# A state-space scan layer: two tiles per scan, decays in SBUF, the carry as a column of the products

## The chip, the cores and the metric

The kernel runs on one core of one Trainium2 chip, as a single launch that computes four image layers one after the other. The metric is the device time of the launch in microseconds (us). A profile of one execution goes with it, taken by the hardware profiler. Its engines are PE (TensorE matrix multiply) with PEld (its weight loads), DVE (VectorE), ACT (ScalarE), POOL (GpSimd) and SP (SyncE, which here only starts DMAs).

## The reference

The input is an image x of 48 channels by 128 x 128 pixels in float32. Each layer normalises x by groups of channels, applies its own operator and adds the result to x: attention over all pixels (layer 0), four directional recurrent sweeps (layer 1), a patchwise convolution through Fourier transforms (layer 2) and a selective scan (layer 3). Only layer 3 matters here:

```python
# tokens: (1, 4096, D) with D = 192: 48 channels x a 2x2 window of pixels
Bm = tokens @ W_B.T + b_B
Cm = tokens @ W_C.T + b_C
dt = jax.nn.softplus(tokens @ W_dt.T + b_dt)
delta = jax.nn.softplus(dt + b_dt)
A = -jnp.exp(A_log)                       # (D, D)

def step(h, inp):                         # over the 4096 tokens
    d_l, u_l, B_l, C_l = inp
    dA = jnp.exp(d_l[:, :, None] * A[None])
    h = dA * h + (d_l * u_l)[:, :, None] * B_l[:, None, :]
    y = jnp.einsum('bdn,bn->bd', h, C_l)
    return (h, y)
```

So there are 192 x 192 independent first-order recurrences over 4096 tokens: h = decay * h + product, where the decay is exp(delta * A) and the product is (delta * u) * B. The state is then contracted with C over n, and a skip term and a constant factor are added.

## The kernel before

Layers 0 to 2 stand first and are not touched. Layer 3 is the function `scan`. The 4096 tokens are cut into four chunks of LC = 1024. The 192 rows d are handled in Q = 96 pairs: two rows d lie on two halves of 64 partitions each, and the 192 states n are three blocks k of 64. A tile is thus 128 partitions by 1024 tokens for one pair and one k. Three pairs (P = 3) make a group of nine tiles, and there are 32 groups (NG) in each chunk: 128 groups and 1152 tiles in all. The buffer `h` holds the nine tiles of a group; the pool `l3_h` has two such buffers.

The loop over groups runs over nine slots, `p, k = divmod(slot, 3)`. This is what it does for a tile:

- At k = 0, SP loads the broadcast rows `dt` (delta) and `du` (delta times u) of the pair from DRAM, and POOL forms the products of all three k with one instruction, `nc.gpsimd.tensor_mul` at line 1497, which writes `h[:, p, ks]` from `du` and `bt` (the B matrix of the chunk). Both inputs and the output lie in SBUF.
- For each slot, ACT computes the decays, `act.activation(dA, dt, AF.Exp, scale=...)`, into `dA`, which lies in PSUM (pool `ps_a`, two buffers).
- DVE runs the recurrence with `nc.vector.tensor_tensor_scan` at line 1504. It reads `dA` from PSUM and the products from `h` in SBUF, and writes the states over the products. Its initial value is the constant 0.0 in the first chunk and the pointer `carry[:, i, k : k + 1]` in the later ones.

A scan therefore waits for its exponential and for the products of its pair. An exponential waits until the scan of two tiles before has read its PSUM buffer. The products of a group wait until the buffer `h` of two groups earlier has been read by everyone.

The contraction with C is hung into the slots of the following group (`contract`, `late`): at slot 1 PE multiplies the finished tiles of `h` with the placed C matrix `cw` into `y` (192 matmuls for each of two parts), at slot 2 ACT copies the last state column of the group to `carry` (`hand_on`), at slots 6 and 7 ACT copies `y` to `ev`, PE picks rows by `sel`, ACT copies them to `ys` at slots 9 and 10, and a DMA stores them to DRAM. `ev` and `ys` come from the pool `l3_e` with two buffers. In the last chunk `finish` adds the results to the image and writes it out. The work that makes the next chunk ready (`prepare`, `part_steps`) is spread over slots 3 and 8; it uses a tile `dd`. `InOrder` (line 48 issues for it) keeps the instructions of ACT and of PE in the order in which the program names them; DVE and POOL have only the waits.

At the start of the layer, `first` prepares chunk 0. It reads the first part of the image from `const["x3"]`, a tile of SBUF that layer 2 fills and that nothing reads afterwards.

Of the kernel before, what the change touches and what calls it, by code (L numbers as in the profile page):

```python
# [19 lines left out]
F32 = mybir.dt.float32  # L20
F16 = mybir.dt.float16
AF = mybir.ActivationFunctionType
ALU = mybir.AluOpType
# [955 lines left out]
def scan(ctx, tc, x3, const, ins, out):  # L979
# [7 lines left out]
    nc = tc.nc  # L987
    act, pe = InOrder(tc, nc.scalar), InOrder(tc, nc.tensor)
    ident = const["ident"]
    so = const["so"]  # L990
    C2 = 2 * C
    D = 4 * C
    L = CH
    NP = 2
    LC = NP * L
# [4 lines left out]
    P = 3  # L1000
    NG = Q // P
    BK = 16
    NB = L // BK // 4

    wp = ctx.enter_context(tc.tile_pool(name="l3_w", bufs=1))
    ap = ctx.enter_context(tc.tile_pool(name="l3_a", bufs=2))
    sp = ctx.enter_context(tc.tile_pool(name="l3_s", bufs=1))
    hp = ctx.enter_context(tc.tile_pool(name="l3_h", bufs=2))
    bp = ctx.enter_context(tc.tile_pool(name="l3_b", bufs=3))
    ep = ctx.enter_context(tc.tile_pool(name="l3_e", bufs=2))  # L1010
    dram = ctx.enter_context(tc.tile_pool(name="l3_y", bufs=1, space=bass.MemoryType.DRAM))
    dram2 = ctx.enter_context(tc.tile_pool(name="l3_dd", bufs=2, space=bass.MemoryType.DRAM))
    ps_a = ctx.enter_context(tc.tile_pool(name="l3_pa", bufs=2, space=PSUM))
# [30 lines left out]
    nc.gpsimd.memset(cw, 0.0)  # L1044

    carry = wp.tile([128, Q, 3], F32, name="carry")
    yd = dram.tile([D, T], F32, name="yd")
    yu = dram.tile([D, T], F32, name="yu")
    yu_by = yu.rearrange("(c a b) l -> a c b l", a=2, b=2)
# [4 lines left out]
    def prepare(ci):  # L1054
# [8 lines left out]

        def first():

            t = hp.tile([128, P, 3, LC], F32, name="h")[0:C2].rearrange("c p k l -> c (p k l)")
            e, w, dd = t[:, 0 : 2 * LC], t[:, 2 * LC : 4 * LC], t[:, 4 * LC : 8 * LC]
            e, w = (v.rearrange("c (b l) -> c b l", b=2) for v in (e, w))
            dd = dd.rearrange("c (b s l) -> c b s l", b=2, s=2)
            ln = ct[0:C2, 0:2, :]  # L1070
            for part in range(NP):
                us.append(ap.tile([C2, 2, L], F32, name="xn"))
            for part, x in enumerate(us):
                xi = rows(const["x3"][:, part, :]).rearrange("c i (j b) -> c i j b", b=2)
                xo = x.rearrange("c b (i j) -> c i j b", j=64)
                act.activation(xo, xi, AF.Identity, bias=so[:, 1:2], scale=so[:, 0:1])

            def both(lhsT, m):
                t = ps_a.tile([128, LC], F32, name="dA")
                for part, x in enumerate(us):  # L1080
                    for b in range(2):
                        pe.matmul(
                            t[0:m, part * L : (part + 1) * L],
                            lhsT=lhsT(b),
                            rhs=x[:, b, :],
                            start=(b == 0),
                            stop=(b == 1),
                        )
                return t[0:m]

            def split(b, z):
                bias = bdt[:, b : b + 1]
                act.activation(e[:, b], z, AF.Abs, bias=bias)
                nc.vector.tensor_scalar(dd[:, b, 1], z, bias, 0.0, ALU.add, ALU.max)

            def take_both(out, t, bias):
                act.activation(out, t, AF.Identity, bias=bias)

            for again in range(2):
                for b in range(2):  # L1100
                    split(b, dd[:, b, 0] if again else both(lambda i: wdt[:, i, b, :], C2))
                for b in range(2):
                    act.activation(e[:, b], e[:, b], AF.Exp, scale=-1.0)
                    nc.vector.tensor_scalar_add(w[:, b], e[:, b], 1.0)
                for b in range(2):
                    act.activation(ln[:, b], w[:, b], AF.Ln)

                    nc.vector.scalar_tensor_tensor(
                        w[:, b], w[:, b], 1.0, e[:, b], ALU.subtract, ALU.subtract
                    )  # L1110
                    nc.vector.tensor_sub(e[:, b], dd[:, b, 1], w[:, b])
                if again == 0:
                    tables()
                    for k in range(2):
                        take_both(bt[:, k], both(lambda i: wb[:, i, k, :], 128), bb[:, k : k + 1])
                for b in range(2):
                    nc.vector.tensor_add(dd[:, b, 0], e[:, b], ln[:, b])
            take_both(bt[:, 2], both(lambda i: wb[:, i, 2, :], 128), bb[:, 2:3])
            for b in range(2):
                for part, x in enumerate(us):  # L1120
                    cols = slice(part * L, (part + 1) * L)
                    nc.vector.tensor_mul(dd[:, b, 1, cols], dd[:, b, 0, cols], x[:, b, :])
                for i in range(2):
                    half = slice(i * C, (i + 1) * C)
                    (act if i else nc.sync).dma_start(rep_by[i][:, b], dd[half, b])
            for k in (2, 0, 1):
                take_both(ct[:, k], both(lambda i: wc[:, i, k, :], 128), bc[:, k : k + 1])
            for part, x in enumerate(us):
                for b in range(2):
                    act.activation(  # L1130
                        w[:, b, part * L : (part + 1) * L], x[:, b], AF.Copy, scale=dp[:, b : b + 1]
                    )
            for i in range(2):
                act.dma_start(yu_by[i][:, :, 0:LC], w[i * C : (i + 1) * C])
# [142 lines left out]
        if ci == 0:  # L1277
            first()
            for f in placing:
                f()  # L1280
            return {"bt": bt, "rep": rep}, [], []
        else:
            dd0 = sp.tile([C2, 2, 2, L], F32, name="dd")
            steps += part_steps(0) + part_steps(1)

        held = {}
# [29 lines left out]
    def contract(h, g, ci):  # L1316
# [8 lines left out]
        def products(part):  # L1325
            def f():
                y[part] = ps_y.tile([128, NB * P * BK], F32, name="y")
                for q in range(NB):
                    for k in range(3):
                        for j in range(4):  # L1330
                            m = (j * NP + part) * NB + q
                            pe.matmul(
                                y[part][
                                    j * 32 : (j + 1) * 32, q * P * BK : (q + 1) * P * BK
                                ].rearrange("m (p t) -> m p t", t=BK),
                                lhsT=cw[:, k, m, :],
                                rhs=h[:, :, k, m * BK : (m + 1) * BK],
                                start=(k == 0),
                                stop=(k == 2),
                            )  # L1340

            return f

        def hand_on():
            act.copy(carry[:, g * P : (g + 1) * P, :].unsqueeze(3), h[:, :, :, LC - 1 : LC])

        def take(part):
            return lambda: act.copy(ev[:, part], y[part])
# [106 lines left out]
        }  # L1455

    ready, steps, place = prepare(0)
    late = {}
    for ci in range(NCK):
        r = ready  # L1460
        if ci:
            steps = []
        for g in range(NG):
            h = hp.tile([128, P, 3, LC], F32, name="h")
            for slot in range(3 * P):
                p, k = divmod(slot, 3)
                i = g * P + p
# [2 lines left out]
                if (g, slot) == (1, 1):  # L1470
                    while place:
                        place.pop(0)()
                    if ci + 1 == NCK:
                        ct = sp.tile([128, 3, LC], F32, name="ct").rearrange("c k l -> c (k l)")
                        dd = sp.tile([C2, 2, 2, L], F32, name="dd").rearrange(
                            "c b s l -> c (b s) l"
                        )
                        for n in range(4):
                            yy = ct[:, n * 2 * D : (n + 1) * 2 * D]
                            ends.append((yy.rearrange("t (s e) -> t s e", e=D), dd[0:C, n]))  # L1480
# [7 lines left out]
                if k == 0:  # L1488
# [6 lines left out]
                            )  # L1495
                    for ks in [slice(0, 3)] if ci or i else [slice(n, n + 1) for n in range(3)]:
                        nc.gpsimd.tensor_mul(  # L1497
                            h[:, p, ks],
                            du.unsqueeze(1).to_broadcast([128, ks.stop - ks.start, LC]),
                            r["bt"][:, ks],  # L1500
                        )
                dA = ps_a.tile([128, LC], F32, name="dA")
                act.activation(dA, dt, AF.Exp, scale=a[:, k, i : i + 1])
                nc.vector.tensor_tensor_scan(  # L1504
                    h[:, p, k, :],
                    dA,
                    h[:, p, k, :],
                    carry[:, i, k : k + 1] if ci else 0.0,
                    ALU.mult,
                    ALU.add,  # L1510
                )
            late = {n - 3 * P: fs for n, fs in late.items()}
            for n, fs in contract(h, g, ci).items():
                late.setdefault(n, []).extend(fs)
# [232 lines left out]
```

## Time and profile before

| | us |
|---|---|
| median of 3 runs | 7599.12 |
| lowest, highest run | 7595.06, 7599.31 |
| profiled execution | 7597.49 |
| its span, first to last instruction | 7595.7 |
| first product of line 1497 starts | 4924.70 |
| first scan of line 1504 starts | 4935.89 |
| last scan of line 1504 starts | 7573.4 |
| PE busy in the whole span | 6125.8 |
| ACT busy in the whole span | 4410.3 |
| DVE busy in the whole span | 3378.7 |
| POOL busy in the whole span | 2792.3 |

The span is what the profile covers; the device time of the same execution is 1.8 us more. The busy times of the whole span mix four layers with different limits, so a change in layer 3 is read from its own stage, which takes the last third, from about 4925 us to the end. In the cost groups each line gives the source line, the engine, the operation, the tiles written and read, the shapes and the count, then the busy time in us and the mean of one in ns, and after the second bar the idle time of the engine just before such instructions, and what ended it. Line 48 is the helper that issues for ACT and PE, so these are told apart by the names of their tiles.

### The profile page before, as it was taken

How to read it: one execution, taken by the hardware profiler on the slowest of the kernel's cores; microseconds unless marked ns; L12 is line 12 of the kernel's file. 1: busy time of each engine (PE TensorE's matmuls, PEld its weight loads, DVE VectorE, ACT ScalarE, POOL GpSimd, SP SyncE). 2: the span in 40 equal slices, each digit the busy share in tenths (PEclk: the TensorE clock that was granted, in tenths of full speed). 3: DMA queues.
4: the chain of work that ended last, by engine and by line, in shares of the span. 5: the costliest groups of instructions: out<-in, count | busy, mean ns of one | idle time of the engine just before them, and what ended most of it. 6: DMA issues, size and time to landing. Idle time of an engine off the chain costs nothing.

```text
span 7595.7 us, 203249 instructions
## 1 busy us (share of the span) xinstructions
PE 6125.8 (81%) x93756; PEld 3162.8 (42%) x93756; DVE 3378.7 (44%) x2497; ACT 4410.3 (58%) x4868; POOL 2792.3 (37%) x574
## 2 busy tenths in 40 slices
PE   7999999999999999999988889755545545554555
PEld 3333333333333333333367755334334343343444
DVE  8300000000000000000022234499999999999998
ACT  2566666666666666666625003366666667666665
POOL 0000000000000000000000022299999999999998
PEclk9999999999999999999999999876767767776666
DMA  3000000000000000000000011166556665656775
GB/s 66 8 4 4 4 3 4 4 4 3 4 4 3 4 4 4 3 4 4 4 1 17 1 33 37 46 160 165 158 158 167 156 160 154 164 159 164 177 181 150
DMA packets 182350, 484.85 MB, mean 64 GB/s; under 512 B 35859, under 2 KB 67778, under 8 KB 179506
## 3 DMA queue, kind: packets, MB, share of 16 engines
q1 hardware_dynamic: 175471, 464.69, 24.0%
q8 instruction: 735, 12.04, 0.7%
q10 hardware_dynamic: 6019, 7.09, 0.4%
q14 instruction: 125, 1.02, 0.0%
HBM read 428.03 MB, written 22.02 MB: 59 GB/s over the span
## 4 chain that ended last, share of the span: by engine, by line
PE 58%; DVE 24%; issue 7%; POOL 4%; ACT 2%; DMA 1%; SPq 0%; DVEq 0%; POOLq 0%; ACTq 0%
PE s L48 23%; PE acc L48 23%; DVE h L1504 20%; PE p L678 6%; POOL h L1497 3%; PE y L48 2%; DVE xb L48 1%; DVE xa L48 1%; DMA du<-rep 1%; PE pp L48 1%; PE pc L48 1%; PE po L48 1%; ACT dA L48 1%; DVE y L48 0%; POOL y L901 0%
## 5 line engine op out<-in xcount | busy, mean ns | idle before, releaser
L48 ACT ACTIVATE e<-s,absT 128x1024 f32<-128x1024 f32 x2048 | 2279.2, 1115 | 1197.5 <-PE s L48 1196.7
L1497 POOL TENSOR_TENSOR h<-du,bt 128x3072 f32<-128x3072 f32 (+1 forms) x386 | 2560.0, 6672 | 83.2 <-DMA du<-rep 62.1
L48 PE MATMUL s<-xa,xb 49*64 49x512 f32 x16384 | 2133.9, 589 | 10.6 <-DVE xb L271 10.6
L48 PE MATMUL acc<-e,xb 64*64 64x512 f32 x16384 | 2131.9, 588 | 0.0
L1504 DVE TENSOR_TENSOR_SCAN h<-dA,carry,h 128x1024 f32<-128x1024 f32 x864 | 1939.8, 2329 | 43.3 <-ACT dA L48 27.2
L48 ACT ACTIVATE dA<-dt,a 128x1024 f32<-128x1024 f32 x1152 | 1287.3, 1118 | 867.5 <-DVE h L1504 856.4
L48 PE MATMUL y<-h,cw 128*32 128x48 f32 x49152 | 886.2, 244 | 933.2 <-issue 499.0
L366 DVE TENSOR_TENSOR both<-o 128x512 f32<-128x512 f32 x32 | 22.2, 693 | 3078.6 <-ACT o L48 3078.6
L614 POOL MEMSET xa<- 48x128 f32 x1 | 0.3, 326 | 3523.5 <-PE acc L48 3523.5
L48 PEld LDWEIGHTS y<-h,cw 128*32 128x32 f32 x49152 | 796.5, 138 | 1057.8 <-issue 653.1
L48 PEld LDWEIGHTS s<-xa,xb 49*64 49x64 f32 x16384 | 643.9, 132 | 1129.9 <-issue 587.3
L48 PEld LDWEIGHTS acc<-e,xb 64*64 64x64 f32 x16384 | 643.1, 132 | 1118.9 <-issue 1096.0
L1504 DVE TENSOR_TENSOR_SCAN h<-dA,h 128x1024 f32<-128x1024 f32 x288 | 633.9, 2270 | 44.8 <-ACT dA L48 36.0
L48 PE MATMUL yz<-ev,sel 128*8 128x48 f32 x4096 | 193.5, 260 | 280.0 <-ACT ev L48 274.3
L48 PEld LDWEIGHTS yz<-ev,sel 128*8 128x8 f32 x4096 | 162.7, 106 | 338.3 <-ACT ev L48 305.9
L678 PE MATMUL p<-xb,l_w 112*112 112x129 f32 x1524 | 233.6, 289 | 42.6 <-DVE xb L48 42.5
L678 PE MATMUL p<-xa,l_w 112*112 112x129 f32 x1524 | 232.2, 288 | 41.9 <-DVE xa L48 41.9
L699 POOL TENSOR_TENSOR xb<-xb,xa 48x2048 f32<-48x2048 f32 (+2 forms) x10 | 44.7, 4465 | 559.0 <-DVE xa L48 559.0
L678 PEld LDWEIGHTS p<-xb,l_w 112*112 112x112 f32 x1524 | 181.9, 177 | 94.1 <-DVE xb L48 94.1
L661 ACT COPY xa<-xb 48x128 f32<-48x128 f32 x256 | 107.3, 419 | 194.5 <-issue 136.0
L678 PEld LDWEIGHTS p<-xa,l_w 112*112 112x112 f32 x1524 | 180.6, 176 | 93.3 <-DVE xa L48 93.3
L48 PE MATMUL pc<-wt,xa 128*128 128x288 f32 x768 | 198.8, 416 | 7.4 <-DMA xa<-xa 7.4
(186 smaller groups left out, 3349.7 us busy)
## 6 DMA issues: line engine op xcount, KB each, us to landing
du<-rep SPq DMA_DIRECT2D x768, 256.0 KB
dt<-rep SPq DMA_DIRECT2D x768, 256.0 KB
rep<-dd SPq DMA_DIRECT2D x24, 192.0 KB
yd<-ys ACTq DMA_DIRECT2D x256, 12.0 KB
rest<-xa SPq DMA_DIRECT2D x90, 38.0 KB
band<-band SPq DMA_DIRECT2D x8, 414.4 KB
xa<-in_x_dram SPq DMA_DIRECT2D x8, 384.0 KB
rest<-band SPq DMA_DIRECT2D x96, 32.0 KB
```

The lines of the kernel that those rows point to most:

```text
L48: ins = method(*args, **kwargs).ins
L366: nc.vector.tensor_add(self.both, o[:, 0], o[:, 1])
L614: nc.gpsimd.memset(b[64:K, lines, E + W - 1 : E + W], 0.0)
L661: nc.scalar.copy(u[at : at + C, :, y], t[0:C, E + h, E : E + W])
L678: nc.tensor.matmul(p, lhsT=w[0:K, which, i, :], rhs=state[0:K, 2 * i : 2 * i + L], start=False, stop=(i == 2),)
L699: nc.gpsimd.tensor_add(xr, xr, u[0:C, x : x + xr.shape[2], E : E + H].rearrange("c w h -> c h w"),)
L1497: nc.gpsimd.tensor_mul(h[:, p, ks], du.unsqueeze(1).to_broadcast([128, ks.stop - ks.start, LC]), r["bt"][:, ks],)
L1504: nc.vector.tensor_tensor_scan(h[:, p, k, :], dA, h[:, p, k, :], carry[:, i, k : k + 1] if ci else 0.0, ALU.mult, ALU.add,)
```

## The change

Three things are changed in `scan`. One scan instruction now covers two neighbouring tiles of `h`, and a single one is used for the ninth tile of a group and for the first pair of the first chunk. The decays go to two SBUF tiles `dA0` and `dA1` of two times 1 + 1024 columns, used in turn, whose first columns are zero. And each tile of `h` has one more column ahead of its products: ACT copies the carry of the pair there at the start of the group, for all nine tiles in one instruction. At this column the decay is zero, so that the recurrence forgets what came before and takes over the carry, and the scan's initial value is always the constant 0.0. The carry is cleared at the start.

To make room in SBUF, `l3_e` has one buffer instead of two, and `dd` uses the tile `const["x3"]`.

```diff
-    ep = ctx.enter_context(tc.tile_pool(name="l3_e", bufs=2))
+    ep = ctx.enter_context(tc.tile_pool(name="l3_e", bufs=1))
...
     carry = wp.tile([128, Q, 3], F32, name="carry")
+    nc.vector.memset(carry, 0.0)
+    decays = [wp.tile([128, 2, 1 + LC], F32, name=f"dA{i}") for i in range(2)]
+    for t in decays:
+        nc.vector.memset(t[:, :, 0:1], 0.0)
+    dd0 = const["x3"].rearrange("c b (s l) -> c b s l", s=2)
...
-            dd0 = sp.tile([C2, 2, 2, L], F32, name="dd")
...
-                                rhs=h[:, :, k, m * BK : (m + 1) * BK],
+                                rhs=h[:, :, k, 1 + m * BK : 1 + (m + 1) * BK],
...
-            act.copy(carry[:, g * P : (g + 1) * P, :].unsqueeze(3), h[:, :, :, LC - 1 : LC])
+            act.copy(carry[:, g * P : (g + 1) * P, :].unsqueeze(3), h[:, :, :, LC:])
...
-    late = {}
+    late, behind = {}, 0
...
-            h = hp.tile([128, P, 3, LC], F32, name="h")
+            h = hp.tile([128, P, 3, 1 + LC], F32, name="h")
+            act.copy(h[:, :, :, 0:1], carry[:, g * P : (g + 1) * P, :].unsqueeze(3))
...
                         nc.gpsimd.tensor_mul(
-                            h[:, p, ks],
+                            h[:, p, ks, 1:],
                             du.unsqueeze(1).to_broadcast([128, ks.stop - ks.start, LC]),
                             r["bt"][:, ks],
                         )
-                dA = ps_a.tile([128, LC], F32, name="dA")
-                act.activation(dA, dt, AF.Exp, scale=a[:, k, i : i + 1])
-                nc.vector.tensor_tensor_scan(
-                    h[:, p, k, :],
-                    dA,
-                    h[:, p, k, :],
-                    carry[:, i, k : k + 1] if ci else 0.0,
-                    ALU.mult,
-                    ALU.add,
-                )
+                if not behind:
+                    decays.append(decays.pop(0))
+                act.activation(decays[0][:, behind, 1:], dt, AF.Exp, scale=a[:, k, i : i + 1])
+                behind += 1
+
+                if behind == 2 or slot == 3 * P - 1 or not (ci or i):
+                    scanned = h.rearrange("n p k l -> n (p k) l")[:, slot + 1 - behind : slot + 1]
+                    nc.vector.tensor_tensor_scan(
+                        scanned.rearrange("n k l -> n (k l)"),
+                        decays[0][:, 0:behind].rearrange("n k l -> n (k l)"),
+                        scanned.rearrange("n k l -> n (k l)"),
+                        0.0,
+                        ALU.mult,
+                        ALU.add,
+                    )
+                    behind = 0
```

More of the change, by code (lines that the diff above doesn't have):

```diff
@@ L1064, in first @@
         def first():
-            t = hp.tile([128, P, 3, LC], F32, name="h")[0:C2].rearrange("c p k l -> c (p k l)")
+            t = hp.tile([128, P, 3, 1 + LC], F32, name="h")[0:C2].rearrange("c p k l -> c (p k l)")
             e, w, dd = t[:, 0 : 2 * LC], t[:, 2 * LC : 4 * LC], t[:, 4 * LC : 8 * LC]
@@ L1474, in scan @@
                         ct = sp.tile([128, 3, LC], F32, name="ct").rearrange("c k l -> c (k l)")
-                        dd = sp.tile([C2, 2, 2, L], F32, name="dd").rearrange(
-                            "c b s l -> c (b s) l"
-                        )
+                        dd = dd0.rearrange("c b s l -> c (b s) l")
                         for n in range(4):
@@ L1501, in scan @@
                         )
-                dA = ps_a.tile([128, LC], F32, name="dA")
-                act.activation(dA, dt, AF.Exp, scale=a[:, k, i : i + 1])
-                nc.vector.tensor_tensor_scan(
-                    h[:, p, k, :],
-                    dA,
-                    h[:, p, k, :],
-                    carry[:, i, k : k + 1] if ci else 0.0,
-                    ALU.mult,
-                    ALU.add,
-                )
+                if not behind:
[13 more added lines that the diff above has]
+                    behind = 0
             late = {n - 3 * P: fs for n, fs in late.items()}
```

## Prediction

> **What bounds the kernel now.** I read the forty slices first, then the cost groups, then the timeline and the two scan-layer lines by source, and the chain of waits last. The slices give the stage that the change can reach:
>
> ```profile
> PE   7999999999999999999988889755545545554555
> DVE  8300000000000000000022234499999999999998
> ACT  2566666666666666666625003366666667666665
> POOL 0000000000000000000000022299999999999998
> ```
>
> From slice 26 on (26 x 189.9 = 4937 us) it is the scan layer, and it fills both DVE and POOL; ACT is at six tenths and PE at five. The window over this stage says so in numbers (columns: stretch, its length, then busy time and count of PE, PEld, DVE, ACT, POOL):
>
> ```profile
> 4924.70:7569.00 2644.30, 1410.38 (x53780) 1084.58 (x53782) 2566.96 (x1150) 1722.91 (x2048) 2573.93 (x392) 0.69 0.63 164
> 7200.00:7400.00 200.00, 117.05 (x4344) 96.76 (x4338) 200.00 (x90) 125.15 (x150) 197.81 (x31) 0.67 0.70 178
> ```
>
> DVE 2567 and POOL 2574 of 2644 us: two engines side by side, each 97% full. Their instructions:
>
> ```profile
> L1497 POOL TENSOR_TENSOR h<-du,bt 128x3072 f32<-128x3072 f32 (+1 forms) x386 | 2560.0, 6672 | 83.2 <-DMA du<-rep 62.1
> L1504 DVE TENSOR_TENSOR_SCAN h<-dA,carry,h 128x1024 f32<-128x1024 f32 x864 | 1939.8, 2329 | 43.3 <-ACT dA L48 27.2
> L48 ACT ACTIVATE dA<-dt,a 128x1024 f32<-128x1024 f32 x1152 | 1287.3, 1118 | 867.5 <-DVE h L1504 856.4
> L1504 DVE TENSOR_TENSOR_SCAN h<-dA,h 128x1024 f32<-128x1024 f32 x288 | 633.9, 2270 | 44.8 <-ACT dA L48 36.0
> ```
>
> The exponentials wait for the scans (856 us), not the reverse. The timeline from 7197 us (start, duration, instruction, count) gives the spacing, which the means overstate since neighbours overlap:
>
> ```profile
> 7197.42 53.49 POOL L1497 TENSOR_TENSOR h<-du,bt 128x3072 f32<-128x3072 f32 x8
> 7199.07 47.16 DVE L1504 TENSOR_TENSOR_SCAN h<-dA,carry,h 128x1024 f32<-128x1024 f32 x21
> ```
>
> So 53.49/8 = 6.69 us for a product of three tiles, 47.16/21 = 2.246 us for a scan with the carry as a scalar operand. In chunk 0, where the initial value is a constant, the timeline has 18 scans in 39.37 us from 4935.89: 2.187 us. A group of nine tiles is thus 3 x 6.69 = 20.1 us of POOL and 9 x 2.246 = 20.2 us of DVE, in parallel. The last view that matters is how steady a scan is while POOL never rests (minimum/median/maximum in ns):
>
> ```profile
> L1504 DVE TENSOR_TENSOR_SCAN h<-dA,carry,h x864: 2323/2327/2351, 5592.6 to 7573.4; 128x1024 f32<-128x1024 f32 x173
> L1497 POOL TENSOR_TENSOR h<-du,bt x386: 2341/6702/6817, 4924.7 to 7560.1; 128x3072 f32<-128x3072 f32 x191, 128x1024 f32<-128x1024 f32 x2
> ```
>
> The reader is to see that the slowest of 864 scans is 1.2% above the fastest: today the two engines don't touch each other. The chain of waits agrees on what ends last (DVE and POOL each appear as the links):
>
> ```profile
> PE s L48 23%; PE acc L48 23%; DVE h L1504 20%; PE p L678 6%; POOL h L1497 3%; PE y L48 2%; DVE xb L48 1%; DVE xa L48 1%; DMA du<-rep 1%; PE pp L48 1%; PE pc L48 1%; PE po L48 1%; ACT dA L48 1%; DVE y L48 0%; POOL y L901 0%
> ```
>
> [...] in the scan stage every DVE instruction beside a running product is a scan from PSUM. [...] 2187/1024 = 2.14 ns an element, against 1216 ns for a 96x1024 two-input subtraction on DVE.
>
> **The change, part by part.** Profiled execution: 7597.49 us, span 7595.7, so 1.8 us outside it; the median of the runs is 7599.12, 0.02% above, and I predict on the profiled one.
>
> *Scans in pairs.* The built program has 511 scans of 2050 columns and 130 of 1025 in place of 1152 of 1024. [...] Total 511 x 4.325 + 130 x 2.19 = 2210 + 285 = 2495 us, against 2574 busy now. Saved on DVE alone: about 0.7 us a group.
>
> *What POOL makes of it.* The products keep their number, their size and their two inputs; only the output is shifted by one column. By spacing, 383 x 6.68 + 3 x 2.37 = 2565 us, and six products of line 1221, 14 us: 2579 us. Even with DVE free, POOL alone fills the stage. A DVE saving can bring at most the difference of the group times, 20.2 - 20.05, in the 96 groups of chunks 1 to 3: 15 us.
>
> *Decays in SBUF.* This is the term that decides. The scan now reads two SBUF tensors (decays and h), and its partner POOL, which reads du and bt from SBUF, is busy 97% of the time. [...] Then the stage takes the sum and not the maximum: 2579 + 2495 = 5074 us. [...] I take 38 us[...]: 5112 us. POOL starts at 4924.7, so the last scan ends at 10037. The tail after it (7573.4 + 2.33 to 7595.7) stays 20 us: 10057, with 1.8 us outside 10059.
>
> *Edits hidden either way.* The exponentials go to SBUF: 1050 ns for a 96x1024 one there, 1118 ns into PSUM, between -0.07 and +0.1 us each, on an engine with 867 us of idle before them. The 128 copies of the carry column ahead of the products, at 191 ns (as carry<-h), are 24 us of ACT; the copy waits for the matmuls of two groups earlier, long done, and behind it stand exponentials with two pairs of slack. POOL's first product of a group waits, in the built order, for the same matmuls and the same carry<-h copy as now, not for the new copy, so POOL is not tied to ACT. A scan of columns 2 and 3 now waits for the second product of its group; POOL is a product ahead, so nothing. One buffer in place of two for ys and ev: each is free ten slots before its next use. SP's queue is unchanged. Three memsets ahead of line 1094, under 1 us.
>
> **The rivals.**
> *No lock for a scan*[...]. For: the trace can't exclude it. [...] Then POOL is the bound and the gain is the 15 us above, less waits from coarser scans of at most 10: 7585, from 7575 to 7600. This is the side of no slowdown, and it decides if a paired scan lasts 4.4 us beside a running product.
> *The interface is shared access by access.* A group's products read 3 x 3072 x 2 = 18432 values per partition in 20.05 us; if this fills the interface, the scans' 9225 more make 27657 x 20.05 / 18432 = 30.1 us a group, plus 10 us in 128 groups: 1285 us more, 8880. [...]
> *The change does what it says and nothing comes of it* is the first rival's upper half: DVE gets 79 us lighter and POOL, as long as before, sets the end.
>
> **How the numbers follow.** Serialised 0.77, shared 0.09, no lock 0.14. The prediction is the first: 10060 us. Its own range is 9950 to 10260. Leaving out only the no-lock case and the ends, the range runs from the shared case's 8850 to 10300. Chances, with 0.2% (15 us) as the least that a measurement of this kernel can tell: no lock splits into 0.06 faster and 0.08 within; all else, 0.86, is slower.
>
> **What would show it.** Right: POOL and DVE busy or blocked in turn, a group of 40 us in place of 20, product or scan durations stretched by the other's length (products toward 11 us, or paired scans toward 11), ACT and PE shares in the stage halved, and every stage before 4880 us unchanged. Shared access would show both stretched by about half. Wrong: paired scans at 4.3 to 4.5 us beside products at 6.7 us, and a group still at 20 us.

## The result, and the profile after

| | before, us | after, us |
|---|---|---|
| median (4 runs each) | 7599.22 | 9994.59 |
| lowest, highest | 7595.06, 7602.96 | 9988.34, 10002.11 |
| span of the profiled execution | 7595.7 | 10000.3 |
| first product starts | 4924.70 | 4929.65 |
| first scan starts | 4935.89 | 4940.84 |

The ratio is 1.315, with a 95% interval of 1.3132 to 1.3167: the kernel became 31.5% slower. All but some 7 us of it lies between the first and the last scan. The slices of the page after (here a slice is 250 us, so the layer begins in the 20th) show what happened to the two engines that were both full:

```profile
DVE  8000000000000002234599999999999999999999
ACT  2666666666666663302333333333333333333333
POOL 0000000000000001022377677777777777767776
```

DVE is full for twice as long, ACT at half its former share, and POOL no longer full. The cost groups of the same page (busy us and mean ns, then idle before and what ended it) say that the instructions themselves got longer:

```profile
L1514 DVE TENSOR_TENSOR_SCAN h<-dA,h 128x2050 f32<-128x2050 f32 (+1 forms) x641 | 4969.5, 7824 | 90.2 <-ACT dA L48 60.9
L1502 POOL TENSOR_TENSOR h<-du,bt 128x3072 f32<-128x3072 f32 (+1 forms) x386 | 3681.4, 9563 | 1289.5 <-PE y L48 810.1
L48 ACT ACTIVATE dA<-dt,a 128x1024 f32<-128x1024 f32 x1152 | 1303.9, 1147 | 2816.5 <-DVE h L1514 2724.2
```

The product of three tiles has the same shape as before and its mean went from 6672 to 9563 ns; nothing that it computes was changed. The instructions that touch `h` in 30 us of the stage (minimum/median/maximum in ns) show the pattern, and two paired scans a little later, with no product beside them, show the free length:

```profile
L1514 DVE TENSOR_TENSOR_SCAN h<-dA,h x4: 2261/10834/10869, 9017.5 to 9049.9; 128x2050 f32<-128x2050 f32 x3, 128x1025 f32<-128x1025 f32 x1
L1502 POOL TENSOR_TENSOR h<-du,bt x3: 8179/10777/10832, 9015.9 to 9034.9; 128x3072 f32<-128x3072 f32 x3
L1514 DVE TENSOR_TENSOR_SCAN h<-dA,h x2: 4405/4417/4429, 9053.5 to 9057.9; 128x2050 f32<-128x2050 f32 x2
```

Three of the four scans and two of the three products last 10.8 us, and on each engine a record begins as soon as the one before it has ended (products at 9024.1 and 9034.9; scans at 9028.3 and 9039.1). So the records of the two engines overlap, but their ends alternate. The product that begins at 9024.1 meets a running scan, which ends at 9028.4; the product ends 6.5 us after that, at 9034.9. The scan that begins at 9028.3 meets that product and ends 4.3 us after it, at 9039.2. A recorded duration here holds the wait for the other engine: the wait is no idle time in this profile. I call this exclusion the lock, and one scan and one product in the alternation a turn. Over the whole layer, a product that waited ends 6.47 us after the scan that it waited for (median of 360), a paired scan that waited 4.29 us after the product (273), and a turn takes 10.76 us. Free of each other, scans follow every 4.32 us and products every 6.61 us in this same kernel. POOL's idle time of 1290 us costs nothing: DVE is busy or blocked almost all the time (90 us idle before its scans), and most of POOL's waits (810 us) are for a free `h`.

### The profile page after: what moved, and what is told of

Its sections match the earlier page's. It is cut to its first block, busy times and chain, and to the rows that moved or that the text cites. A ratio compares the mean times of both kernels' runs of the same rounds, so it can differ in the third digit from the quotient of the medians.

```text
span 10000.3 us, 203085 instructions
## 1 busy us (share of the span) xinstructions
PE 6185.0 (62%) x93756; PEld 3182.7 (32%) x93756; DVE 5774.7 (58%) x1989; ACT 4410.3 (44%) x4996; POOL 3924.4 (39%) x574
## 4 chain that ended last, share of the span: by engine, by line
PE 42%; DVE 35%; issue 17%; ACT 1%; POOL 1%; DMA 0%; ACTq 0%; SPq 0%; DVEq 0%; POOLq 0%
DVE h L1514 32%; PE acc L48 18%; PE s L48 18%; PE p L678 5%; DVE xb L48 1%; PE y L48 1%; DVE xa L48 1%; ACT dA L48 1%; PE po L48 1%; PE pc L48 1%; DVE y L48 0%; POOL y L900 0%; POOL y L901 0%; POOL y L899 0%; PE f L48 0%
## 5 line engine op out<-in xcount | busy, mean ns | idle before, releaser
L1514 DVE TENSOR_TENSOR_SCAN h<-dA,h 128x2050 f32<-128x2050 f32 (+1 forms) x641 | 4969.5, 7824 | 90.2 <-ACT dA L48 60.9
L1502 POOL TENSOR_TENSOR h<-du,bt 128x3072 f32<-128x3072 f32 (+1 forms) x386 | 3681.4, 9563 | 1289.5 <-PE y L48 810.1
L48 PE MATMUL y<-h,cw 128*32 128x48 f32 x49152 | 944.0, 255 | 2956.6 <-DVE h L1514 2486.5
L48 PEld LDWEIGHTS y<-h,cw 128*32 128x32 f32 x49152 | 867.7, 148 | 3070.5 <-issue 2171.5
L48 PEld LDWEIGHTS s<-xa,xb 49*64 49x64 f32 x16384 | 616.4, 132 | 1156.8 <-issue 601.1
L48 PEld LDWEIGHTS acc<-e,xb 64*64 64x64 f32 x16384 | 615.7, 132 | 1145.9 <-issue 1122.6
L48 DVE TENSOR_TENSOR xb<-p,mask 112x129 f32<-112x129 f32 x254 | 74.5, 293 | 268.6 <-PE p L678 259.2
L48 DVE TENSOR_TENSOR xa<-p,mask 112x129 f32<-112x129 f32 x254 | 74.5, 293 | 244.1 <-PE p L678 244.1
```

The costliest lines, as they stand in the source:

```text
L48: ins = method(*args, **kwargs).ins
L1502: nc.gpsimd.tensor_mul(h[:, p, ks, 1:], du.unsqueeze(1).to_broadcast([128, ks.stop - ks.start, LC]), r["bt"][:, ks],)
L1514: nc.vector.tensor_tensor_scan(scanned.rearrange("n k l -> n (k l)"), decays[0][:, 0:behind].rearrange("n k l -> n (k l)"), scanned.rearra ...
```

## The experiments

Where no ratio is given, the time is that of one execution; executions of one kernel differ here by up to some 18 us.

**Which part of the change is it?** First, the decays alone, in the kernel before:

```diff
-                dA = ps_a.tile([128, LC], F32, name="dA")
+                dA = da.tile([128, LC], F32, name="dAs")      # a pool of two buffers in SBUF
...
-    ep = ctx.enter_context(tc.tile_pool(name="l3_e", bufs=2))
+    ep = ctx.enter_context(tc.tile_pool(name="l3_e", bufs=1))
...
-            dd0 = sp.tile([C2, 2, 2, L], F32, name="dd")       # now the tile const["x3"]
```

> The kernel before with one part of the change alone: the decays of each single tile go to an SBUF tile instead of PSUM (with the two edits that make room). No pairs, no carry column. Theory, exclusive lock: scans and products run in turn, 288 x 2.187 + 864 x 2.246 = 2570 us of scans plus 384 products at 6.45 us (what a blocked product costs after the change) = 2477 us, plus some 100 us of idle and other POOL work; total about 10100 us (9950 to 10250), each scan that meets a product about 8.7 us long. Rival, the loss comes from the pairs, the carry column or the single buffers: within 30 us of 7600.

Measured: 9995.71 us (the kernel before 7598.52 beside it). This is the changed kernel's time to within 2 us, with no pair and no carry column in it. The scans of chunks 1 to 3 and their products:

```profile
L1503 DVE TENSOR_TENSOR_SCAN h<-dAs,carry,h 128x1024 f32<-128x1024 f32 x864 | 3762.6, 4432 | 13.3 <-ACT dAs L48 13.3
L1496 POOL TENSOR_TENSOR h<-du,bt 128x3072 f32<-128x3072 f32 x383 | 3140.9, 8225 | 1755.4 <-PE y L48 1317.1 <-DMA du<-rep 259.9 <-DVE h L1503 75.6
```

Of all 1152 scans, 366 last 8 to 9 us, the rest 2.3 with a handful of longer ones: one scan in three waits for a product, and the mean doubles. The total expected was 100 us too high.

Second, the rest of the change but for the pairs, with the decays back in PSUM: single scans, padded tiles, carry column and carry copies, single buffers.

```diff
-                act.activation(decays[0][:, behind, 1:], dt, AF.Exp, scale=a[:, k, i : i + 1])
+                dA = ps_a.tile([128, LC], F32, name="dA")
+                act.activation(dA, dt, AF.Exp, scale=a[:, k, i : i + 1])
...
+                nc.vector.tensor_tensor_scan(
+                    h[:, p, k, 1:], dA, h[:, p, k, 1:], h[:, p, k, 0:1], ALU.mult, ALU.add,
+                )
```

> The changed kernel with the decays of single tiles back in PSUM and one scan for each tile; its carry column (read as the scan's pointer), the carry copies, the padded tiles and the single buffers stay. Theory, the lock is the whole of the loss: within 0.3% of 7599 us (7580 to 7620). Rival, a part of the loss sits in the other edits: the time would lie above 7650 us.

Measured: 7607.46 us against 7597.84, ratio 1.001 (1.0001 to 1.0018). These edits cost a tenth of a per cent. The first run showed that the place of the decays by itself, without pairs, makes the whole of the loss.

**Is it POOL, and is it POOL's reading?** The changed kernel, with POOL writing as much but reading nothing:

```diff
-                        nc.gpsimd.tensor_mul(h[:, p, ks, 1:], du.unsqueeze(1).to_broadcast(...), r["bt"][:, ks])
+                        nc.gpsimd.memset(h[:, p, ks, 1:], 0.0)
```

> The changed kernel with POOL's product replaced by a memset of the same output, so that POOL writes as much and reads nothing; the products are left out. Theory, the lock binds only a POOL instruction that reads SBUF: scans run free at 4.32 us a pair, 19.5 us a group, total about 7480 us (7440 to 7540). Rival 1, a scan of two SBUF inputs is slow by itself: about 10000 us. Rival 2, any POOL instruction takes the lock: a memset of 3072 columns takes about half of the 5.22 us of the one of 6144, so 384 x 2.6 = 1000 us more, about 8480 us.

Measured: 7675.77 us. Paired scans from SBUF, beside a POOL that writes SBUF:

```profile
L1510 DVE TENSOR_TENSOR_SCAN h<-dA,h 128x2050 f32<-128x2050 f32 x511 | 2229.0, 4422 | 197.8 <-ACT carry L48 133.0 <-ACT dA L48 64.7
L1502 POOL MEMSET h<- 128x3072 f32 x381 | 998.5, 2659 | 1709.6 <-PE y L48 1581.3 <-ACT dA L48 67.4 <-DMA yu<-h 50.8
```

A paired scan lasts 4422 ns in the mean; 279 of the 511 have a memset beside them, and their median is 4402 ns. So the scan is not slow by itself, and POOL's writes don't hold it: rivals 1 and 2 fall. ACT's writes of the decays to SBUF, which are here as in the changed kernel, don't hold it either.

The same run holds a test in small. POOL still has six instructions that read SBUF, those of line 1228, which work on the next chunk. Exactly six scans, three paired and three single, are longer than the others (6.5 us and 4.4 us), and each of them meets one of these six. The first of them, with the three scans around it:

```profile
5124.25 4.84 POOL L1228 TENSOR_TENSOR x_first<-x_first,xn 96x1024 f32<-96x1024 f32 x1 [6.00 <-ACT x_first L48]
L1510 DVE TENSOR_TENSOR_SCAN h<-dA,h x3: 4397/4430/6516, 5122.5 to 5133.3; 128x2050 f32<-128x2050 f32 x3
```

But the time lies 200 us above the expected 7480, and the first line says where: DVE idles 198 us before these scans, for ACT. I come back to it.

With a POOL instruction that reads one SBUF tensor:

```diff
+                        nc.gpsimd.tensor_copy(h[:, p, ks, 1:], r["bt"][:, ks])
```

> The changed kernel with POOL's product replaced by a copy of the B matrix to the same output, so that POOL reads one SBUF tensor instead of two; the factor du is left out. With c for the copy's own length (between the 2.6 us of a memset and the 6.7 us of the product): theory, any reading instruction of POOL takes the lock: scans stretched by c, total about 4940 + 2495 + 384 x c + 100, from 8500 to 10050 us. Rival, only a POOL instruction with two inputs contends: about 7480 us.

Measured: 8444.17 us, just below the expected span, since the copy is shorter than I allowed for. Scans and copies:

```profile
L1510 DVE TENSOR_TENSOR_SCAN h<-dA,h 128x2050 f32<-128x2050 f32 x511 | 2841.9, 5616 | 34.5 <-ACT dA L48 32.3 <-ACT carry L48 2.2
L1502 POOL COPY h<-bt 128x3072 f32<-128x3072 f32 x383 | 2149.8, 5648 | 1297.0 <-PE y L48 1220.2 <-ACT dA L48 27.5 <-DMA dt<-rep 26.0
```

In turns both last 6.9 us, and a turn takes 6.82 us: 4.28 for the scan, 2.54 for the copy. One read is enough here: beside such a copy a paired scan lasts up to 6.97 us, and 4.4 us beside the memset. The rival falls.

**Is it held for a whole instruction?** The product in three instructions of one tile:

```diff
-                    for ks in [slice(0, 3)] if ci or i else [slice(n, n + 1) for n in range(3)]:
+                    for ks in [slice(n, n + 1) for n in range(3)]:
```

> The changed kernel with each product of three tiles issued as three instructions of one tile. Theory, the lock is held for a whole instruction and handed over at its end: a paired scan never waits longer than about one small product, so it lasts at most about 4.4 + 2.3 = 6.7 us (now 10.8), while the sum stays: 1152 x (2.3 - 0.2) + 2495 = 4910 us, total about 9950 us (9700 to 10150). Rival, the ports are shared in time slices or access by access: scan durations stay where the sharing puts them, 10.8 us for many, whatever the instruction's size.

Measured: 9995.39 us, again the same total, with other durations:

```profile
L1502 POOL TENSOR_TENSOR h<-du,bt 128x1024 f32<-128x1024 f32 x1152 | 5012.2, 4390 | 54.8 <-DMA du<-rep 47.3 <-PE y L48 7.5
L1514 DVE TENSOR_TENSOR_SCAN h<-dA,h 128x2050 f32<-128x2050 f32 x511 | 3373.1, 6602 | 1107.8 <-POOL h L1502 1107.8
```

Of the 511 paired scans 509 last 6.5 to 7 us and one 27 us; none of the 10.8 us scans is left. The wait inside a scan follows the length of the other's instruction (6.6 us in the mean beside small products, 10.8 us beside large ones), as a hand-over at its end gives. The rest of DVE's wait is now plain idle time, 1108 us for products that aren't ready, and the sum stays.

**One tile in nine.** The kernel before with `dA = (da if slot == 8 else ps_a).tile(...)`:

> The kernel before with the decays of the ninth tile of each group alone in SBUF (with the two edits that make room), the other eight in PSUM. Theory, exclusive lock: POOL gives up 2.2 us a group, 20.0 + 2.2 = 22.2 us a group if DVE's wait for the running product is made good by its slack, at most 20.2 + 6.5 = 26.7 us if every such scan waits for a whole product: from 256 to 830 us more, 7850 to 8430 us. Rival, the loss grows with the share of scans alone: 2395 / 9 = 266 us, 7865 us, with scans that wait half a product.

Measured: 7954.56 us, 358 more than the 7596.76 beside it: 2.8 us a group for one 2.2 us scan, or 15% of the loss for 11% of the scans. It lies within the span of the theory but doesn't decide much; it shows that even this small dose isn't free while both engines are full.

**Where the 200 us without the lock went.** The run without POOL reads, with a third decay tile:

```diff
-    decays = [wp.tile([128, 2, 1 + LC], F32, name=f"dA{i}") for i in range(2)]
+    decays = [wp.tile([128, 2, 1 + LC], F32, name=f"dA{i}") for i in range(3)]
...
+    bu = ctx.enter_context(tc.tile_pool(name="l3_bu", bufs=1))      # du, which POOL doesn't read here
```

> The kernel without POOL reads (7675.77 us, 150 to 200 us above the sum of its scans) with three decay tiles in place of two (one du buffer in place of three makes the room; the products are left out). In that run DVE waits about 1.4 us at each group's edge for the exponentials, which stand behind the carry copy, the ys copies and a DMA issue on ACT with only two decay tiles. Theory, the third decay tile hides this: about 7500 us (7470 to 7540). Rival, ACT's own order makes the wait whatever the buffers: about 7675 us.

Measured: 7598.82 us, so 77 us of the 200 come back. DVE's idle time before paired scans fell:

```profile
L1511 DVE TENSOR_TENSOR_SCAN h<-dA,h 128x2050 f32<-128x2050 f32 x511 | 2233.9, 4424 | 121.0 <-ACT dA L48 89.6 <-ACT carry L48 31.1
```

Neither theory is right alone: the buffers make some of the wait. The rest is probably ACT's fixed order, since in this run the copies of `y` to `ev` wait 569 us for PE in the same queue as the exponentials; that was not tried by itself.

**Is there something to gain?** Three runs ask what DVE's relief is worth while POOL is as long as before. In the kernel before, with the initial value always 0.0 (the carry is left out):

> The kernel before with the scan's initial value 0.0 in every chunk; the carry between chunks is left out. This takes 0.059 us from each of 864 scans, so 51 us of DVE, without touching POOL. Theory, POOL's 20.0 us a group is the bound directly behind DVE's 20.2: about 15 us less, 7584 us (7575 to 7592). Rival, DVE is the bound by itself: 51 us less, 7548 us.

Measured: 7575.62 us, ratio 0.997 (0.9958 to 0.9982), 22 us less. It is nearer to POOL as the bound than to 51 us. The gain that the change could have had at all, with POOL's products as they are, is thus an estimated 0.3%.

A version with a carry column and decays in PSUM, two tiles of 1025 columns side by side behind one result tile:

```diff
+    shared = ps_a.tile([128, 5 * L], F32, name="dA")
+    y0 = shared[:, 0 : NB * P * BK]
+    decays = [shared[:, NB * P * BK + n * (1 + LC) : NB * P * BK + (n + 1) * (1 + LC)] for n in range(2)]
...
+                nc.vector.tensor_tensor_scan(h[:, p, k, :], dA, h[:, p, k, :], 0.0, ALU.mult, ALU.add)
```

> A version meant to beat both: carry column and constant initial value as in the change, but single scans of 1025 columns whose decays lie in PSUM behind a zero column[...]. One SBUF input, so no lock. Theory: DVE 9 x 2.19 = 19.7 us a group, POOL 20.0 sets the end: 7584 us (7572 to 7595). Rival, the carry copy and the narrower exponentials' order on ACT leave a wait at each group's edge: above 7610 us.

Measured: 9629.77 us, ratio 1.2672 (1.2655 to 1.269), far from what was expected. The trace has no lock in it (all 1152 scans last 2291 to 2296 ns) but a chain:

```profile
7006.34 2.29 DVE L1514 TENSOR_TENSOR_SCAN h<-dA,h 128x1025 f32<-128x1025 f32 x1 [1.25 <-ACT dA L48]
7008.67 1.12 ACT L48 ACTIVATE dA<-dt,a 128x1024 f32<-128x1024 f32 x1 [2.43 <-DVE h L1514]
7009.82 2.29 DVE L1514 TENSOR_TENSOR_SCAN h<-dA,h 128x1025 f32<-128x1025 f32 x1 [1.19 <-ACT dA L48]
7012.15 1.12 ACT L48 ACTIVATE dA<-dt,a 128x1024 f32<-128x1024 f32 x1 [2.36 <-DVE h L1514]
```

Each exponential waits for the scan just before it, not for the one before that: 3.48 us a tile. Over the layer a tile takes 4.04 us; the exponentials also wait 778 us for PE, whose results lie in the same PSUM tile. The two decay tiles are neighbouring columns of that one tile, and the built program seems to order accesses to it more coarsely than by columns; that reason was not tried by itself.

Last, the kernel before with the carry brought in by ACT, which leaves nothing of the computation out:

```diff
+                if ci:
+                    act.activation(
+                        h[:, p, k, 0:1], dA[:, 0:1], AF.Identity,
+                        bias=h[:, p, k, 0:1], scale=carry[:, i, k : k + 1],
+                    )
...
-                    carry[:, i, k : k + 1] if ci else 0.0,
+                    0.0,
```

> A version meant to beat both: the kernel before, decays in PSUM and single scans, the initial value always the constant 0.0, and in chunks 1 to 3 ACT adds decay times carry to the first product of each tile (one element a partition, about 0.2 us, 864 of them; the whole computation is kept). Theory: DVE as in the kernel without carry (7575.62 us), ACT has 867 us of idle for 170 us of work, so 7578 us (7570 to 7588). Rival: the exponential, the small instruction and two hand-overs on ACT no longer fit behind one scan, or ACT waits for POOL in its fixed order: 7600 us or more.

Measured: 7587.63 us against 7596.76, ratio 0.9987 (0.998 to 0.9994): faster than both kernels, by 0.13%, at the upper end of what was expected. The small instruction is dearer than my 0.2 us:

```profile
L48 ACT ACTIVATE h<-dA,h,carry 128x1 f32<-128x1 f32 x864 | 303.8, 352 | 91.8 <-POOL h L1497 61.5
L1512 DVE TENSOR_TENSOR_SCAN h<-dA,h 128x1024 f32<-128x1024 f32 x1152 | 2534.2, 2268 | 118.4 <-ACT h L48 77.1 <-ACT dA L48 33.2 <-POOL h L1497 6.7
```

DVE now waits 77 us for it, and its waits before scans add up to 118 us, against 95 us in the run without the carry. The gain is 9 us, less than half of the 22 us there.

## Why the prediction was right, and where it was not

*The bound.* Two full engines side by side: right. It is why the lock costs almost the whole of the other engine's time (the stage went from 2640 us, first scan to end of the last, to 5038; a group takes 39.4 us).

*The lock.* That the scan and the product can't run together was an assumption of mine: in the trace before, every scan beside a product reads its decays from PSUM (2323 to 2351 ns with the carry), so a scan of two SBUF inputs beside a product could not be seen there. It held, and the runs show it in three parts: two SBUF inputs on DVE (decays_alone against all_but_sbuf_decays, 9996 against 7607 us), a POOL instruction that reads (no_pool_reads and pool_one_read, 4.4 us and 6.9 us for a paired scan beside POOL's memset and POOL's copy), and exclusion to the end of the instruction (product_in_thirds, 6.5 to 7 us for 509 of 511 paired scans).

*The sum.* From POOL's start to the end of the last scan I had 5112 us; it was 9978.5 - 4929.65 = 5049. The scans were priced right: 511 x 4.32 + 130 x 2.18 = 2491 us for my 2495. The 4.325 us of a pair was my estimate, for the scans of the trace before all have 1024 columns; at their 2.14 ns a column a pair would take 4.38 us. In the changed kernel a free pair takes 4.32 us and a free single scan 2.18, so (4.32 - 2.18)/1025 = 2.09 ns for each further column. The 38 us on top of the sum, 0.1 us for each of 384 products, were my allowance for the hand-over, which the trace before does not show, and had the wrong sign. A turn costs 10.76 us and not 6.68 + 0.1 + 4.32: a product that waited takes 6.47 us and a paired scan that waited 4.29. Against a free product that is 0.14 us less. A product's fixed part, by the trace before (3 x 2341 - 6702)/2 = 160 ns, would give about this if it passed during the wait; that is an estimate, no run tried it by itself. The whole turn, against mine, makes 384 x 0.34 = 130 us less. No delay shows at a hand-over (6.47 us after waiting, 6.61 free). Against the 130 us stand waits of DVE for ACT that I had priced at nothing, 60.9 + 27.4 + 1.7 - 22.1 (the first, which belongs to the start) = 68 us. 5112 - 4 - 130 + 68 = 5046. The two errors partly cancel: the serialised sum was the right mechanism, but that the total lay within 65 us of the measured median is in part luck.

*What I called hidden.* "Behind it stand exponentials with two pairs of slack" was wrong. The slack is less at a group's edge, where the ninth tile takes a decay tile for itself and the single scan lasts 2.2 us, while ACT has the `ys` copies, a DMA issue and the carry copy in its queue. In the changed kernel the lock hides much of this: DVE is idle for 90 us before its scans, and for 222 us in the run without POOL's reads, which took 7676 us. So the first rival was mis-sized too: 7585 us counted on POOL as the only bound, and a group there took (7654 - 4935)/128 = 21.2 us, above POOL's 20.05. From that run I estimate the change without a lock at some 7680 us, slower than before; no run has both products and no lock.

*The rivals.* Access-by-access sharing, if it were so, would have given an estimated 8880 us, and durations stretched by half; the scans more than double (4.4 to 10.8 us), and the ends alternate. It falls.

*Details.* The first product starts 5 us later than before, where I had under 1 us. The change need not be the reason: product_in_thirds, which is the same up to there, starts its first product at 4923.6 us. The tail after the last scan was 22 us for my 20. `ev` and `ys` are free some eight slots before their next use by the order of the slots, not ten.

## What to carry to other kernels

Before moving an operand of a scan on DVE from PSUM to SBUF, count its SBUF inputs, and look at what POOL does at that time. Here a float32 scan with two of them ran in turn with a POOL instruction that reads SBUF, beside a product (9996 us against 7599 in decays_alone) and beside a copy (8444 us against 7676 with the memset), so the sum of both engines was the price and not the larger. For other instructions of DVE it was not shown. In the changed kernel's profile the wait is mostly no idle time but a longer instruction (a paired scan of 10.8 us for 4.4), longer by what is left of the other engine's instruction. And with two engines equally full, relief of one is worth only the small difference between them (here 22 us, about 0.3%, in no_carry), whatever it saves on its own engine.

## What was not expected of the hardware

A hand-over between the two engines costs no time that can be seen here: a product that waited takes 6.47 us from the scan's end, against 6.61 us for a free one in the same kernel, and a turn (10.76 us) is shorter than a free scan and a free product together (10.93 us).

The turns are not always fair. Six scans of the changed kernel last 24 to 33 us: DVE waits while POOL runs three or four products in a row, each at its free length (26.52/4 = 6.63 us in the first case).

```profile
5298.81 4.86 POOL L1228 TENSOR_TENSOR x_first<-x_first,xn 96x1024 f32<-96x1024 f32 x1 [13.94 <-ACT x_first L48]
5303.63 26.52 POOL L1502 TENSOR_TENSOR h<-du,bt 128x3072 f32<-128x3072 f32 x4
```

In the changed kernel each of the six stands just behind one of the six instructions of line 1228, the only ones of POOL in this stage that cover 96 partitions instead of 128. The number of partitions can't be the whole cause. product_in_thirds has the same six instructions and only one such scan, of 27 us, and there POOL had passed DVE with two small products before the instruction of line 1228 came:

```profile
L1514 DVE TENSOR_TENSOR_SCAN h<-dA,h x1: 27242/27242/27242, 6958.6 to 6958.6; 128x2050 f32<-128x2050 f32 x1
6949.74 15.69 POOL L1502 TENSOR_TENSOR h<-du,bt 128x1024 f32<-128x1024 f32 x5
6965.39 2.33 POOL L1228 TENSOR_TENSOR x_first<-x_first,xn 96x1024 f32<-96x1024 f32 x1
```

The last two of these five products ran while that scan waited. The cause stays open. What it costs was not measured; I estimate little, since the four products of the first case are no longer than free ones (6.63 us against 6.61) and POOL's work is brought forward.
